# Halving six expert answers on VectorE ahead of the transposes, and normalizing layer 0's output on ScalarE

## The chip, the cores and the metric

The kernel runs on one core of a Trainium2 chip. The time is device microseconds from start to end of one execution, as a median of several runs. The engines of the core work in parallel, each through its own list of instructions in order: TensorE (PE) for matrix products and transposes, VectorE (DVE), ScalarE (ACT), GpSimd (POOL) and SyncE (SP), which here only issues transfers.

## What is computed

The reference has two layers on 8192 tokens (128 graphs of 64 nodes) with 256 values each. Each layer is a graph convolution and then a mixture of experts. Only the seam between the layers matters here: what layer 0 does with its six expert answers per token, and all of layer 1's convolution.

```
# layer 0, experts: six of 64 are chosen for a token, scores are their softmax
lattice_out = einsum('bske,bsk->bse', xW, scores)      # six answers, weighted and summed
proj = einsum('bsd,ed->bse', lattice_out, out_w) + out_b
h = x + proj                                           # x: the layer-normed input
ffn = (h - mu) * rsqrt(var + 1e-5) * ln_g + ln_b
x = x_residual + ffn
# layer 1, convolution, on layernorm(x)
h = layer_norm(xn, ln_gamma, ln_beta)
agg = einsum('bij,bjh->bih', adj, h)
x = x + (xn + relu(agg @ W_rel + b_rel + h @ W_root))
# layer 1, experts: two of eight are chosen, then each token's two answers are added
```

## The kernel before

The program has four stages, one after the other:

1. **layer 0's convolution and routing**: each token is written six times into a table in memory, sorted by expert;
2. **layer 0's experts**: pages of 128 rows go through their expert's matrix, are scaled with their score and scattered to `r0.answer`, six rows of 256 values to a token;
3. **the fused pass**: it reads the six answers of each token, adds them up, finishes layer 0, does layer 1's convolution and routes the tokens to layer 1's experts;
4. **layer 1's experts**.

The change is in stage 3 alone. It works in 32 blocks of 256 tokens (two tiles `t` of 128 tokens; a tile's tokens lie on the 128 partitions). The function `staggered` writes the program out as a software pipeline: in step s it calls each function of the list, in the list's order, for block s minus its lag. So step s has `mixture` and `out_proj` of block s+1, `layer_out_h`, `_a`, `_b`, `_c` of block s, `flip_h`, `neighbours`, `convolve_a`, `convolve_b` of block s-1, `residual1_a`, `residual1_b`, `flip3`, `gate1` of block s-2, and `choose1`, `count1`, `place1` of block s-3. Steps 3 to 30 have all of them; those before and after have a part.

For PE, VectorE and ScalarE the order of the program is the order of execution (`manual_schedule`). The issues on SP and POOL are ordered by a scheduler, and each queue works in its order.

What one block goes through, with the lines of the profile:

- `load3` (L801): SP loads the six answers `y` (L804, 1536 KB, two buffers), the normed input `xn1` (L806), the residual `x1` (L808), three buffers each, and two blocks of the adjacency (L492).
- `mixture` (L811): 24 transposes on PE (L818), six to each of the four 128x128 squares of the PSUM tile, the six adding up there, so that sum and transpose are one. ScalarE copies the result to `accT` (L821).
- `out_proj` (L823): one bias product (L826) and the product with `out_w` on PE (L829) into the one buffer `po`.
- `layer_out_h` (L835): VectorE adds `xn1` and gives `h`. `layer_out_a`: VectorE takes mean and variance of `h` (L45, L46, two tiles), ScalarE the root of the variance (L36), and VectorE adds `ln_b` to `x1` (L841).
- `layer_out_b`: on VectorE the reciprocal of the root (L847) and then for each tile two operations on 128x256 elements: L850 takes off the mean and multiplies by `ln_g`, L852 multiplies by the reciprocal and adds `x1`, which gives `x2`. Statistics of `x2` follow (L45, L46) and two roots on ScalarE (L36).
- `layer_out_c`: scale and shift on VectorE (L67, L68, twice, and L866), four operations on ScalarE (`hn` L869, `s` L873).
- `flip_h` (L76, `hT` L882), `neighbours` (L890, `z` L893), `convolve_a` (L898, L901 into the one buffer `pc`) and `convolve_b` (L907): PE, with ScalarE emptying PSUM.
- `residual1_a`: L913 on VectorE gives `x3`, SP writes it out (L914), statistics, root. `residual1_b`: scale and shift on VectorE (L67, L68), then ScalarE writes `xs` (L923, two operations of 512 elements to a partition).
- `flip3` (L76, `xn3T` L930), `gate1` (L936, into the one buffer `pg`), `choose1` (L942, L178 to L183, L251), `count1` (L191), `place1` (L267 to L281), and four scattering transfers from POOL (L287).

The order on VectorE within a step is so: `choose1` (L942 first), `residual1_a`, `layer_out_a`, `residual1_b`, `layer_out_b`, `place1`, `layer_out_c`, and then `layer_out_h` of the next step's block, which its list has first.

`scale_shift` (L62 to L69), which the change calls once more, is the pair of small VectorE operations L67 and L68: the reciprocal of the root, and minus the mean times it.

Of the kernel before, what the change touches and what calls it, by code (L numbers as in the profile page):

```python
# [9 lines left out]
F32 = mybir.dt.float32  # L10
# [5 lines left out]
AF = mybir.ActivationFunctionType  # L16
ALU = mybir.AluOpType
AX = mybir.AxisListType
PSUM = bass.MemoryType.PSUM
P = 128  # L20
# [382 lines left out]
def staggered(n, stages, first=0):  # L403

    for s in range(first + min(lag for lag, _ in stages), n + max(lag for lag, _ in stages)):
        for lag, f in stages:
            if first <= s - lag < n:
                f(s - lag)
# [3 lines left out]
def two_layer_gnn_moe_kernel(ctx: ExitStack, tc: tile.TileContext, a: dict, out: bass.AP):  # L412
    nc = tc.nc
    x_in, adjT = a["x"], a["adjT"]
    N, D = x_in.shape
# [4 lines left out]
    T = 2  # L420
    C = T * P
# [4 lines left out]
    K0 = 6  # L426
# [15 lines left out]
    ops = Ops(nc, small, ident, eps)  # L442

    def load_rows(pool, name):
        t = pool.tile([P, a[name].shape[0]], F32, name="r_" + name)
        nc.scalar.dma_start(out=t, in_=rows_of(a[name]))
        return t
# [31 lines left out]
    def by_tile(ap):  # L479
        return ap.rearrange("(t p) d -> p t d", p=P)  # L480
# [8 lines left out]
    def load_adjacency(b):  # L489
        at = adjacency[b % 4]  # L490
        for g in range(2):
            nc.sync.dma_start(out=at[g * G:(g + 1) * G, :, g * G:(g + 1) * G],  # L492
                              in_=adjT[2 * b * T + g:2 * (b + 1) * T:2].rearrange("t m n -> m t n"))
        return at
# [3 lines left out]
    r0 = Router(tc, const, small, dram, N, D, E0, K0, T, P, 14 * P, 4, "r0")  # L498
# [22 lines left out]
    with tc.tile_pool(name="c0", bufs=1) as c0, \  # L521
# [9 lines left out]
        blocks = [dict() for _ in range(NB)]  # L531
# [247 lines left out]
    with tc.tile_pool(name="c3", bufs=1) as c3, \  # L779
# [5 lines left out]
        ln_g = load_rows(c3, "L0_ffn_ln_g")  # L785
# [11 lines left out]
        blocks = [dict() for _ in range(NB)]  # L797
        pg = pmix.tile([P, T, E1], F32, name="pg")
        r1.begin(counts, work, pmix.tile([P, 2, T, E1], F32, name="pos"))

        def load3(b):  # L801
            B = blocks[b]
            B["y"] = y = work.tile([P, T, K0, D], F32, name="y")
            nc.sync.dma_start(out=y, in_=r0.answer[ts(b, C * K0), :].rearrange("(t p k) d -> p t k d", p=P, k=K0))  # L804
            B["xn1"] = xn1 = work.tile([P, T, D], F32, name="xn1", bufs=3)
            nc.sync.dma_start(out=xn1, in_=by_tile(xn1_dram[b]))  # L806
            B["x1"] = x1 = work.tile([P, T, D], F32, name="x1", bufs=3)
            nc.sync.dma_start(out=x1, in_=by_tile(x1_dram[b]))  # L808
            B["at"] = load_adjacency(b)

        def mixture(b):  # L811

            B = blocks[b]
            pt = psum.tile([P, KD, C], F32, name="ps")
            for k in range(KD):
                for t in range(T):
                    for i in range(K0):
                        nc.tensor.matmul(pt[:, k, ts(t, P)], lhsT=B["y"][:, t, i, ts(k, P)], rhs=ident,  # L818
                                         start=(i == 0), stop=(i == K0 - 1), is_transpose=True)
            B["accT"] = accT = work.tile([P, KD, C], F32, name="accT", bufs=1)  # L820
            nc.scalar.copy(accT, pt)  # L821

# [14 lines left out]
        def layer_out_a(b):  # L837
# [2 lines left out]
            B["rsh"] = ops.spread(B["mvh"])  # L840
            nc.vector.tensor_add(B["x1"], B["x1"], ln_b.unsqueeze(1).to_broadcast([P, T, D]))  # L841

        def layer_out_b(b):
            B = blocks[b]
            h = B["h"]
            mv, rs = B["mvh"], B["rsh"]
            nc.vector.reciprocal(rs, rs)  # L847
            B["x2"] = x2 = work.tile([P, T, D], F32, name="x2")
            for t in range(T):
                nc.vector.scalar_tensor_tensor(h[:, t, :], h[:, t, :], mv[:, t, 0:1], ln_g,  # L850
                                               op0=ALU.subtract, op1=ALU.mult)
                nc.vector.scalar_tensor_tensor(x2[:, t, :], h[:, t, :], rs[:, t:t + 1], B["x1"][:, t, :],  # L852
                                               op0=ALU.mult, op1=ALU.add)
            B["mv2"] = mv = ops.stats(x2)
            B["std2"] = ops.spread(mv)


            B["rs2"] = rs2 = small.tile([P, T], F32, name="rs2")
            ops.std(rs2, mv[:, :, 1], 1e-10, 1.0 + 1e-5)
# [93 lines left out]
        def place1(b):  # L953
            B = blocks[b]
            r1.send(r1.places(b, B["hot"]), B["xs"])

        staggered(NB, (
            (-2, load3),
            (0, layer_out_h),
            (3, choose1),  # L960
            (-1, mixture),
            (1, flip_h),
            (3, count1),
            (2, residual1_a),
            (0, layer_out_a),
            (-1, out_proj),
            (2, residual1_b),
            (1, neighbours),
            (0, layer_out_b),
            (1, convolve_a),  # L970
            (2, flip3),
# [106 lines left out]
```

## Time and profile before

| | us |
|---|---|
| median of 3 runs (2194.39 to 2196.17) | 2195.01 |
| the profiled execution | 2200.25 |
| its span, on which all views below count | 2198.1 |
| stage 1, up to about | 630 |
| stage 2, up to about | 1264 |
| fused pass: first steps, up to L942 of step 3 | 1313.32 |
| fused pass: steps 3 to 30, up to L942 of step 31 | 1629.51 |
| fused pass: last steps, up to stage 4's first transpose | 1672.9 |
| stage 4, up to the end | 2198.1 |

Between the stretch of steps 3 to 30 and the sum over the whole span, the engines were busy so (us):

| | PE | VectorE | ScalarE | POOL |
|---|---|---|---|---|
| whole span | 1945.1 | 1186.6 | 1015.9 | 1182.8 |
| steps 3 to 30 (316.19 us) | 316.19 | 277.15 | 199.75 | 117.41 |

A busy time is the time in which at least one instruction of the engine was under way. An instruction that needs nothing of the one ahead of it may begin before that one has ended, so that a row's mean duration is longer than what the instruction adds to a row of them. The distance between two starts is told in the text as such. The granted clock ("PEclk") is the share of its full speed that PE was given in a stretch.

### The profile page before, as it was taken

What the parts mean: (1) busy time and instruction counts of PE and PEld (TensorE: products, weight loads), DVE (VectorE), ACT (ScalarE), POOL (GpSimd) and SP (SyncE); (2) the same over time, 40 slices, a digit from 0 to 9 for tenths busy, and PEclk for the clock granted to TensorE, in tenths of its full rate; (3) what the DMA queues carried; (4) which work ended last, traced back from release to release, by engine and by line L of the source; (5) the groups of instructions that cost most, each with busy time, mean ns of one, the idle gap of its engine ahead of it and who ended that gap; (6) DMA issues with size and microseconds to landing.
All of it is one profiled execution on the core that took longest, in us unless ns stands there. A gap on an engine that the chain in (4) does not pass through costs nothing. (4 is left out here: it accounts for less than half of the span.)

```text
span 2198.1 us, 37431 instructions
## 1 busy us (share of the span) xinstructions
PE 1945.1 (88%) x10563; PEld 1684.8 (77%) x10564; DVE 1186.6 (54%) x3904; ACT 1015.9 (46%) x2037; POOL 1182.8 (54%) x1178
## 2 busy tenths in 40 slices
PE   3999999999961988998898479999996999999997
PEld 2888888888851877887777368888875888888886
DVE  4688888888873333333333248888882222222221
ACT  2887887777750222222222036666662333333332
POOL 1166676666655777777777703333343444434444
PEclk9999999999985999999999789999997999999999
DMA  8143334443364988767675379888835776666665
GB/s 247 56 133 123 129 131 134 133 133 134 127 214 136 282 254 256 210 202 206 206 206 170 92 277 316 265 265 267 262 124 142 179 170 158 162 157 161 162 160 117
DMA packets 283580, 398.93 MB, mean 181 GB/s; under 512 B 56024, under 2 KB 237416, under 8 KB 283376
## 3 DMA queue, kind: packets, MB, share of 16 engines
q1 hardware_dynamic: 200736, 246.15, 38.3%
q0 software_dynamic: 64800, 136.14, 20.8%
q10 hardware_dynamic: 17840, 14.21, 2.0%
q8 instruction: 93, 1.52, 0.3%
q14 instruction: 111, 0.91, 0.2%
HBM read 223.89 MB, written 177.69 MB: 183 GB/s over the span
## 5 line engine op out<-in xcount | busy, mean ns | idle before, releaser
L287 POOL DMA_INDIRECT r0x<-xs,r0row x384 | 397.7, 1036 | 222.2 <-DVE lat L613 100.7
L294 POOL DMA_INDIRECT r0y<-py_s,px x424 | 417.6, 985 | 143.7 <-DMA r0y<-py_s,px 58.2
L758 PE MATMUL py<-lat,pxT 128*128 x1696 | 411.0, 385 | 40.0 <-DVE py_s L763 22.5
L763 DVE TENSOR_SCALAR py_s<-py,px 128x256 f32<-128x256 f32 x424 | 185.6, 479 | 377.4 <-DMA r0y<-py_s,px 158.5
L302 POOL DMA_INDIRECT out_x<-py_s,px x138 | 214.4, 1554 | 312.1 <-DMA out_x<-py_s,px 184.2
L758 PEld LDWEIGHTS py<-lat,pxT 128*128 128x128 f32 x1696 | 307.2, 191 | 91.0 <-issue 31.2
L745 ACT COPY pxT<-pt 128x512 f32<-128x512 f32 x212 | 124.0, 586 | 440.8 <-PE pt L743 309.5
L1017 ACT ACTIVATE phid<-ph,pw 128x256 f32<-128x256 f32 x276 | 131.0, 475 | 325.3 <-issue 178.4
L1015 PE MATMUL ph<-pxT,pw 128*128 128x256 f32 x1104 | 251.4, 381 | 2.1 <-DMA pw<-in_L_ffn_W1b 2.1
L1034 PE MATMUL py<-fw,phid 128*128 x1104 | 249.9, 379 | 0.6 <-ACT phid L1017 0.6
L591 PE MATMUL ph<-lat 128*128 128x256 f32 x1024 | 233.2, 387 | 17.8 <-DVE lat L613 17.1
L624 PE MATMUL ps<-lat 128*128 128x256 f32 x1024 | 237.1, 380 | 0.0
L1015 PEld LDWEIGHTS ph<-pxT,pw 128*128 128x128 f32 x1104 | 211.0, 191 | 31.4 <-issue 2.5
L591 PEld LDWEIGHTS ph<-lat 128*128 128x128 f32 x1024 | 195.2, 193 | 46.9 <-DVE lat L613 17.4
L1034 PEld LDWEIGHTS py<-fw,phid 128*128 128x128 f32 x1104 | 204.4, 190 | 26.0 <-ACT phid L1017 1.0
L624 PEld LDWEIGHTS ps<-lat 128*128 128x128 f32 x1024 | 192.8, 191 | 24.5
L287 POOL DMA_INDIRECT r1x<-xs,r1row x128 | 129.8, 1014 | 115.7 <-ACT xn3T L930 61.9
L743 PE MATMUL pt<-ident,px 128*128 128x128 f32 x848 | 131.8, 277 | 45.0 <-DMA px<-r0x 44.7
L743 PEld LDWEIGHTS pt<-ident,px 128*128 128x128 f32 x848 | 106.8, 143 | 70.9 <-issue 42.9
L1028 DVE TENSOR_SCALAR p<-p 128x2 f32<-128x2 f32 x69 | 12.0, 174 | 240.1 <-ACT p L1027 240.1
L1037 DVE TENSOR_TENSOR py_s<-py,pb 128x512 f32<-128x512 f32 x69 | 47.7, 692 | 157.0 <-PE py L1034 152.0
L615 ACT ACTIVATE lat<-lat,c_L_gnn_rms_weight 128x256 f32<-128x256 f32 x256 | 105.6, 495 | 47.8 <-DVE lat L613 47.7
(264 smaller groups left out, 2866.7 us busy)
## 6 DMA issues: line engine op xcount, KB each, us to landing
px<-r0x SPq DMA_DIRECT2D x424, 129.0 KB
y<-r0y SPq DMA_DIRECT2D x32, 1536.0 KB
pw<-in_L_ffn_W1b SPq DMA_DIRECT2D x69, 514.0 KB
px<-r1x SPq DMA_DIRECT2D x69, 258.0 KB
x<-x SPq DMA_DIRECT2D x64, 256.0 KB
pb<-in_L_ffn_b SPq DMA_DIRECT2D x69, 128.0 KB
r0x<-r0filler ACTq DMA_DIRECT2D x64, 129.0 KB
lat<-in_x SPq DMA_DIRECT2D x32, 256.0 KB
```

The lines of the kernel that those rows point to most:

```text
L287: i = self.nc.gpsimd.indirect_dma_start(out=self.table[:, :], out_offset=bass.IndirectOffsetOnAxis(ap=row[:, t, k:k + 1], axis=0), in_=xs[ ...
L294: i = self.nc.gpsimd.indirect_dma_start(out=self.answer[:, :], out_offset=bass.IndirectOffsetOnAxis(ap=x[:, self.D:self.D + 1].bitcast(I32 ...
L302: i, d = f"{self.name}add{i}", self.nc.gpsimd.indirect_dma_start(out=self.total[:, :], out_offset=bass.IndirectOffsetOnAxis(ap=x[:, self.D ...
L591: nc.tensor.matmul(ph[:, c, :], lhsT=w1[:, k, ts(2 * j + c, P)], rhs=B["aggT"][:, k, :], start=(k == 0), stop=(k == KD - 1))
L624: nc.tensor.matmul(B["po"][:, t, :], lhsT=B["hT"][:, c, ts(t, P)], rhs=w2[:, c, :], start=False, stop=(t == T - 1 and c == KH - 1))
L743: nc.tensor.transpose(pt[:, k, ts(q, P)], Q["px", q][:, 0, ts(k, P)], ident)
L745: nc.scalar.copy(xT[:, :, :n * P], pt[:, :, :n * P])
L758: nc.tensor.matmul(py[:, q, :], lhsT=Q["xT"][:, k, ts(q, P)], rhs=lat[:, ds(regs["e"][(2 * j + q) % 4], 1), k, :].rearrange("p o d -> p (o ...
L763: nc.vector.tensor_scalar(y[:, q, :], py[:, q, :], px[:, 0, D + 1:D + 2], None, op0=ALU.mult)
L1015: nc.tensor.matmul(ph, lhsT=w[:, k * F1 + c * P:k * F1 + (c + 1) * P], rhs=Q["xT"][:, k, :], start=(k == 0), stop=(k == KD - 1))
L1017: nc.scalar.activation(hid[:, c, :], ph, AF.Relu, bias=w[:, KD * F1 + c:KD * F1 + c + 1], scale=1.0)
L1034: nc.tensor.matmul(py[:, t, :], lhsT=Q["hid"][:, c, ts(t, P)], rhs=fw2[:, ds(regs["e"][i % 4], 1), c, :].rearrange("p o d -> p (o d)"), st ...
```

## The change

`load_y` takes the load of `y` out of `load3` and issues it one step earlier, with three buffers in place of two. `halve`, a new VectorE operation in each step, adds answers 3 to 5 of a block to its answers 0 to 2, in place: 2 x 768 elements on each partition in one instruction. `mixture` then transposes and sums three answers in place of six. `layer_out_n`, also new, forms scale and shift of `h` on VectorE (`scale_shift`) and lets ScalarE normalize `h` in place, a tile at a time. `layer_out_b` has one multiplication by `ln_g` and one addition of `x1`, each over both tiles (128x512), where it had a reciprocal and four operations on 128x256. In the list `layer_out_n` stands behind `residual1_b`, and `halve`, for block s+2, stands behind `neighbours` and right ahead of `layer_out_b`.

```
--- before.py
+++ after.py
@@ -798,10 +798,16 @@
         pg = pmix.tile([P, T, E1], F32, name="pg")
         r1.begin(counts, work, pmix.tile([P, 2, T, E1], F32, name="pos"))
 
+        def load_y(b):
+            blocks[b]["y"] = y = work.tile([P, T, K0, D], F32, name="y", bufs=3)
+            nc.sync.dma_start(out=y, in_=r0.answer[ts(b, C * K0), :].rearrange("(t p k) d -> p t k d", p=P, k=K0))
+
+        def halve(b):
+            y = blocks[b]["y"]
+            nc.vector.tensor_add(y[:, :, :K0 // 2, :], y[:, :, :K0 // 2, :], y[:, :, K0 // 2:, :])
+
         def load3(b):
             B = blocks[b]
-            B["y"] = y = work.tile([P, T, K0, D], F32, name="y")
-            nc.sync.dma_start(out=y, in_=r0.answer[ts(b, C * K0), :].rearrange("(t p k) d -> p t k d", p=P, k=K0))
             B["xn1"] = xn1 = work.tile([P, T, D], F32, name="xn1", bufs=3)
             nc.sync.dma_start(out=xn1, in_=by_tile(xn1_dram[b]))
             B["x1"] = x1 = work.tile([P, T, D], F32, name="x1", bufs=3)
@@ -814,9 +820,9 @@
             pt = psum.tile([P, KD, C], F32, name="ps")
             for k in range(KD):
                 for t in range(T):
-                    for i in range(K0):
+                    for i in range(K0 // 2):
                         nc.tensor.matmul(pt[:, k, ts(t, P)], lhsT=B["y"][:, t, i, ts(k, P)], rhs=ident,
-                                         start=(i == 0), stop=(i == K0 - 1), is_transpose=True)
+                                         start=(i == 0), stop=(i == K0 // 2 - 1), is_transpose=True)
             B["accT"] = accT = work.tile([P, KD, C], F32, name="accT", bufs=1)
             nc.scalar.copy(accT, pt)
 
@@ -840,17 +846,19 @@
             B["rsh"] = ops.spread(B["mvh"])
             nc.vector.tensor_add(B["x1"], B["x1"], ln_b.unsqueeze(1).to_broadcast([P, T, D]))
 
+        def layer_out_n(b):
+            B = blocks[b]
+            h = B["h"]
+            rs, nm = ops.scale_shift(B["mvh"], B["rsh"])
+            for t in range(T):
+                nc.scalar.activation(h[:, t, :], h[:, t, :], AF.Identity, bias=nm[:, t:t + 1], scale=rs[:, t:t + 1])
+
         def layer_out_b(b):
             B = blocks[b]
             h = B["h"]
-            mv, rs = B["mvh"], B["rsh"]
-            nc.vector.reciprocal(rs, rs)
             B["x2"] = x2 = work.tile([P, T, D], F32, name="x2")
-            for t in range(T):
-                nc.vector.scalar_tensor_tensor(h[:, t, :], h[:, t, :], mv[:, t, 0:1], ln_g,
-                                               op0=ALU.subtract, op1=ALU.mult)
-                nc.vector.scalar_tensor_tensor(x2[:, t, :], h[:, t, :], rs[:, t:t + 1], B["x1"][:, t, :],
-                                               op0=ALU.mult, op1=ALU.add)
+            nc.vector.tensor_mul(h, h, ln_g.unsqueeze(1).to_broadcast([P, T, D]))
+            nc.vector.tensor_add(x2, h, B["x1"])
             B["mv2"] = mv = ops.stats(x2)
             B["std2"] = ops.spread(mv)
 
@@ -955,6 +963,7 @@
             r1.send(r1.places(b, B["hot"]), B["xs"])
 
         staggered(NB, (
+            (-3, load_y),
             (-2, load3),
             (0, layer_out_h),
             (3, choose1),
@@ -965,7 +974,9 @@
             (0, layer_out_a),
             (-1, out_proj),
             (2, residual1_b),
+            (0, layer_out_n),
             (1, neighbours),
+            (-2, halve),
             (0, layer_out_b),
             (1, convolve_a),
             (2, flip3),
```

In the changed kernel's lists of instructions each step of PE has 12 transposes fewer. VectorE's order within a full step is: `choose1`, `residual1_a`, `layer_out_a`, the pair L67, L68 of `residual1_b`, the same pair of `layer_out_n`, the halving, the multiplication, the addition, the statistics of `x2`, `place1`, `layer_out_c`, `layer_out_h`. ScalarE's is: `accT`, `hT` twice, two roots, `xs` twice, the two normalizations of `h`, `z`, two roots, `xn3T`, `hn` twice, `s` twice.

More of the change, by code (lines that the diff above doesn't have):

```diff
@@ L799, in two_layer_gnn_moe_kernel, with load_y, halve @@
         r1.begin(counts, work, pmix.tile([P, 2, T, E1], F32, name="pos"))
+        def load_y(b):
+            blocks[b]["y"] = y = work.tile([P, T, K0, D], F32, name="y", bufs=3)
+            nc.sync.dma_start(out=y, in_=r0.answer[ts(b, C * K0), :].rearrange("(t p k) d -> p t k d", p=P, k=K0))
+        def halve(b):
+            y = blocks[b]["y"]
+            nc.vector.tensor_add(y[:, :, :K0 // 2, :], y[:, :, :K0 // 2, :], y[:, :, K0 // 2:, :])
         def load3(b):
             B = blocks[b]
-            B["y"] = y = work.tile([P, T, K0, D], F32, name="y")
-            nc.sync.dma_start(out=y, in_=r0.answer[ts(b, C * K0), :].rearrange("(t p k) d -> p t k d", p=P, k=K0))
             B["xn1"] = xn1 = work.tile([P, T, D], F32, name="xn1", bufs=3)
@@ L816, in mixture @@
                 for t in range(T):
-                    for i in range(K0):
+                    for i in range(K0 // 2):
                         nc.tensor.matmul(pt[:, k, ts(t, P)], lhsT=B["y"][:, t, i, ts(k, P)], rhs=ident,
-                                         start=(i == 0), stop=(i == K0 - 1), is_transpose=True)
+                                         start=(i == 0), stop=(i == K0 // 2 - 1), is_transpose=True)
             B["accT"] = accT = work.tile([P, KD, C], F32, name="accT", bufs=1)
@@ L841, in layer_out_a, with layer_out_n @@
             nc.vector.tensor_add(B["x1"], B["x1"], ln_b.unsqueeze(1).to_broadcast([P, T, D]))
+        def layer_out_n(b):
+            B = blocks[b]
+            h = B["h"]
+            rs, nm = ops.scale_shift(B["mvh"], B["rsh"])
+            for t in range(T):
+                nc.scalar.activation(h[:, t, :], h[:, t, :], AF.Identity, bias=nm[:, t:t + 1], scale=rs[:, t:t + 1])
         def layer_out_b(b):
@@ L845, in layer_out_b @@
             h = B["h"]
-            mv, rs = B["mvh"], B["rsh"]
-            nc.vector.reciprocal(rs, rs)
             B["x2"] = x2 = work.tile([P, T, D], F32, name="x2")
[L849 to L853, printed above, removed]
+            nc.vector.tensor_mul(h, h, ln_g.unsqueeze(1).to_broadcast([P, T, D]))
+            nc.vector.tensor_add(x2, h, B["x1"])
             B["mv2"] = mv = ops.stats(x2)
@@ L957, in two_layer_gnn_moe_kernel @@
         staggered(NB, (
+            (-3, load_y),
             (-2, load3),
@@ L967, in two_layer_gnn_moe_kernel @@
             (2, residual1_b),
+            (0, layer_out_n),
             (1, neighbours),
+            (-2, halve),
             (0, layer_out_b),
```

## The prediction

> **What bounds the kernel now.** First the 40 slices, to see where the fused pass lies and how full each engine is there.
>
> ```profile
> PE   3999999999961988998898479999996999999997
> DVE  4688888888873333333333248888882222222221
> ```
>
> A slice is 54.95 us, so slices 24 to 29 are the pass: PE is full, and VectorE at 8 tenths is not far behind. Second, the steady part alone, from L942 of step 3 to L942 of step 31 (columns: us, then busy us and instructions of PE, PE's weight loads, VectorE, ScalarE, POOL; granted clock, DMA share, GB/s).
>
> ```profile
> 1313.32:1629.51 316.19, 316.19 (x2074) 277.13 (x2073) 277.15 (x1232) 199.75 (x421) 117.41 (x136) 1.00 0.79 260
> ```
>
> 28 steps, 316.19 / 28 = 11.29 us each, with PE busy for all of it. VectorE is busy for 9.90 us of a step. Whether the other 1.39 us are free is what decides this case, so third VectorE's groups in twenty of these steps (busy us, mean ns; then idle time ahead of them and its cause), with one group from stage 1.
>
> ```profile
> L852 DVE SCALAR_TENSOR_TENSOR x<-h,bn_sd,x 128x256 f32<-128x256 f32 x40 | 19.4, 485 | 1.4
> L850 DVE SCALAR_TENSOR_TENSOR h<-h,bn_mv,r_L_ffn_ln_g 128x256 f32<-128x256 f32 x40 | 18.9, 472 | 0.0
> L841 DVE TENSOR_TENSOR x<-x,r_L_ffn_ln_b 128x512 f32<-128x512 f32 x20 | 13.2, 658 | 0.0
> L942 DVE TENSOR_TENSOR logits<-pg,r_L_ffn_bg 128x16 f32<-128x16 f32 x20 | 3.5, 175 | 12.5 <-PE pg L936 12.5
> ...
> L601 DVE TENSOR_TENSOR lat<-lat 128x1024 f32<-128x1024 f32 x27 | 33.7, 1249 | 22.9 <-ACT lat L594 22.9
> ```
>
> Only L942 waits for another engine: 12.5 / 20 = 0.63 us in a step, for `gate1`. The rest of the 1.39 us are seams between small dependent operations that come again in any order. VectorE's list is therefore 11.29 - 0.63 = 10.67 us long, against PE's 11.29: it is the next bound, and 0.63 us is all it can take.
>
> Fourth, one step in order of time (start, us). I count from L942 at 1437.53 as zero.
>
> ```profile
> 1442.75 0.16 DVE L68 SCALAR_TENSOR_TENSOR bn_nm<-bn_mv,bn_rs 128x2 f32<-128x2 f32 x1
> 1442.83 0.16 DVE L847 RECIPROCAL bn_sd<-bn_sd 128x2 f32<-128x2 f32 x1
> 1442.90 0.46 DVE L850 SCALAR_TENSOR_TENSOR h<-h,bn_mv,r_L_ffn_ln_g 128x256 f32<-128x256 f32 x1
> ...
> 1444.72 0.42 DVE L45 BATCH_NORM_STATS2 bn_st<-x 128x6 f32<-128x256 f32 x1
> ...
> 1447.51 0.69 DVE L835 TENSOR_TENSOR h<-po,xn 128x512 f32<-128x512 f32 x1
> ```
>
> ```profile
> 1443.00 1.52 ACT L923 ACTIVATE xs<-x,bn_nm,bn_rs 128x512 f32<-128x512 f32 x2 [0.60 <-DVE bn_nm L68]
> 1444.71 0.59 ACT L893 COPY z<-pz 128x512 f32<-128x512 f32 x1 [0.20 <-PE pz L890]
> ...
> 1447.09 0.59 ACT L930 COPY xn3T<-ps 128x512 f32<-128x512 f32 x1 [0.63 <-PE ps L76]
> 1447.58 1.09 ACT L869 ACTIVATE hn<-x,bn_nm,bn_rs 128x256 f32<-128x256 f32 x2
> ```
>
> L68 of `residual1_b` ends at 5.38, the statistics of `x2` (L45) begin at 7.19, L835 ends at 10.67. ScalarE starts `xs` as soon as L68 is done and is busy with it until 6.99.
>
> **The change part by part.** *PE*: 24 transposes take 2.67 us (chain view, L818), so 12 give back 1.33: PE's step becomes 9.96 us. Since VectorE can only give 0.63 of that back before it binds, the other 0.70 are worth nothing as they stand.
>
> *VectorE, the four operations*: from L850's start to L45's is 1.82 us. In their place stand a multiplication and an addition on 128x512, each dependent on the one before; L841 has that form at 0.66, and a dependent follower starts 0.04 after the end (L850 to L852: 0.50 for 0.46). 2 x 0.70 = 1.40, a gain of 0.42. *Scale and shift of h*: the pair L67, L68 takes 0.27 from start to start here, in place of one reciprocal at 0.07: a loss of 0.20.
>
> *The halving*: 1536 elements to a partition, an operation that the trace does not have. From below: L841's 658 ns for 512 and 393 ns for the 256 of L563 give 265 per 256, so 1.72 us. From above: L601's 1249 for 1024 and 699 for 512 give 550 per 512, so 1.80. It is L601's kind of addition, but without that one's chain; I take 1.75. Its successor can start 0.08 before its end, as L67 does behind L841.
>
> *The new wait*: the multiplication needs `h` from ScalarE, and in ScalarE's list the two normalizations come behind both `xs`. `xs` still starts at 5.47 and blocks until about 6.95; two operations of the form of L869 take 1.09; `h` is there at 8.05. On VectorE the pair of `layer_out_n` ends its issue at 5.57 and the halving lasts to 7.32, so VectorE stands for 0.73 us. The halving is thus wholly hidden under ScalarE's 5.47 to 8.05, and would be up to 2.48 us; without that cover it costs 1.67. Behind the waiting multiplication are queued the statistics of `x2`, `place1` (POOL's sends wait for it, but POOL is busy for 117.41 / 28 = 4.2 us of a step), `layer_out_c` (`hn`, next step's `flip_h`), `layer_out_h` and the next L942.
>
> So: multiplication at 8.05, addition 8.75, statistics 9.45 in place of 7.19, that is 2.26 later, and VectorE's list ends at 10.67 + 2.26 = 12.93. That is the new step, if nothing else ends later. The other candidate is the way to L942 by PE: last statistics done at 10.61, both roots on ScalarE, which stand ahead of `xn3T` in its list, `xn3T` 11.10 to 11.69, `gate1` 1.06, L942 at 12.84. The two are level, VectorE ahead by 0.1. ScalarE's step grows by 1.09 to 8.2 us and does not bind.
>
> *PE's clock*: PE now has about 3 us of gaps in a step, the largest, some 2.2 us, ahead of `gate1`. What gaps do shows at the end of the pass (same columns as above):
>
> ```profile
> 1630.00:1631.00 1.00, 0.00 (x0) 0.00 (x0) 0.88 (x8) 1.00 (x3) 0.76 (x1) 1.00 0.38 128
> ...
> 1632.00:1633.00 1.00, 1.00 (x4) 0.79 (x3) 0.93 (x5) 0.00 (x0) 0.70 (x2) 0.50 0.39 139
> ```
>
> After 1.05 us without work the granted clock went to 0.50 for some 3.3 us; after 0.82 and 0.71 us again. A `gate1` at half clock (1657.17) took 1.88 in place of 1.06, and by the way over PE a step would then be 13.66, 0.73 more. Bounds: nothing (clock stays, or drops after `gate1`) to 0.73 in every step. A gap of 2.2 us must pull the clock down in most steps, but a slow PE also closes its own gap in the next step; I take 0.3. The Trainium skill, "TensorE: Matmul & The Clock Gate", section "Why this matters for your kernels", advises against PE-idle gaps above about 3 us between bursts, since a whole idle window throttles. By that rule the 2.2 us would cost nothing and the sum would be 8 us lower; the rows above, where 1.05 us sufficed, speak against it.
>
> *Loads*: SP issues as many transfers as before, `y` a step earlier. With three buffers one is free when `mixture` of three blocks before is done, and the halving needs it two steps and 4 us later, some 30 us; the slowest `y` in the chain view landed in 7.84 us. The DMA share of 0.79 falls with a longer step. Nothing, where it was covered before too. In the first steps `y` binds; the halving there delays (1.75), fewer transposes and an earlier `y` of block 2 advance: zero, by -2 to +2.
>
> **Sum.** Steps 3 to 30: 28 x (12.93 - 11.29) = 45.9. Clock: 28 x 0.3 = 8.4. Step 31 (10.63 us now, no halving, but the same wait): 12.84 - 10.63 = 2.2. Together 56.5 us, a span of 2198.1 + 56.5 = 2254.6. The profiled execution's span is 3.1 above the median of the runs, so the median is 2195.0 + 56.5 = 2251.5; I say 2251.
>
> **Rivals.** *A, ScalarE's part hides*: the normalizations are ready when the halving ends. The multiplication then starts at 7.24, statistics at 8.64, and the step is 12.12: 28 x 0.83 + 1.4 = 25, so 2220. For it: ScalarE stands idle for 0.60 us ahead of `xs`, so its list is not full there. Against it: that idle time ends with the very L68 that `xs` needs, and `xs`, 1.5 us long, is ahead of the normalizations in a list that is kept in order. *B, faster*: VectorE's additions, halving included, fit into the 0.63 us that L942 waits, and PE's relief shows: at most 28 x 0.63 = 17.6 less, 2177. It needs less than 0.63 more on VectorE's list and my rows give 2.26; L841 would have to be off threefold. *C, the clock dominates*: every `gate1` at half clock, and the slow stretch (half of 3.3 us lost) at worst not covered: 0.73 to 1.6 in a step, 2263 to 2288. For it: `gate1` directly follows the gap. Against it: PE has 3 us of slack for all but `gate1`. *D, the edit has no effect on time*, since what PE gains VectorE loses: it would need 0.63 sharp.
>
> **Numbers.** Forecast 0.72, A 0.12, C 0.11, B 0.04, D 0.01. A measurement of this kernel tells about 0.2% from no change. The bounds of the unknown clock alone span 2243 to 2264; half of A's and C's cases added, 2222 to 2270. Slower 0.94, faster 0.04, same 0.02.
>
> **What would show it.** In the changed profile's steady steps: a distance of 12.9 to 13.4 us between L950s (the old L942); PE busy about 10 us of it; the multiplication L860 waiting some 0.7 us for ScalarE's `h`, and the halving at 1.7 to 1.8. A step near 12.1 with L860 not waiting is A; stretches of granted clock 0.5 in each step with L950 waiting for `gate1` are C; L950 still waiting for a PE that is busy throughout is B. I am wrong if VectorE's list can be packed closer than its start-to-start distances before.

## The result, and the profile after

| | before | after |
|---|---|---|
| median, us (range, runs) | 2195.59 (2194.39 to 2197.61, 4) | 2250.22 (2247.74 to 2258.79, 4) |
| ratio of after to before, 95% interval | | 1.0255 [1.0225, 1.0285] |
| profiled execution / its span | 2200.25 / 2198.1 | 2258.79 / 2257.0 |
| L942 (after: L950) of step 3 | 1313.32 | 1311.92 |
| the same of step 31 | 1629.51 | 1676.18 |
| steps 3 to 30 / mean step | 316.19 / 11.29 | 364.26 / 13.01 |
| step 31 | 10.63 | 12.80 |

The kernel is 2.55% slower. The forecast was 2251. First the 40 slices of the page; the third row is the clock granted to PE.

```profile
PE   3999999999934989998997388888886999999997
DVE  4688888888872333333333388888882222222221
PEclk9999999999966999999999698989887999999999
```

The fused pass is now about slices 23 to 30, of 56.4 us each. PE has gone from full to 8 tenths, and its clock has dents; VectorE has not become fuller in exchange: it stood at 8 tenths before and stands there now. Neither engine is full, so the pass is held by waits between engines. The steady part alone, from L950 of step 3 to L950 of step 31 (us, then busy us and instructions of PE, PE's weight loads, VectorE, ScalarE and POOL; granted clock, DMA share, GB/s):

```profile
1311.92:1676.18 364.26, 318.50 (x1737) 272.83 (x1735) 317.87 (x1232) 226.94 (x476) 113.74 (x136) 0.90 0.71 222
```

Here are 48.07 us more than before in 28 steps. VectorE is busy 317.87 / 28 = 11.35 us of a mean step of 13.01, and PE 11.37: fewer instructions of PE (1737 in place of 2074) take as long as before, at a mean clock of 0.90 in place of 1.00. VectorE's groups in 19 of these steps (busy us, mean ns; then idle time ahead of them and its cause):

```profile
L807 DVE TENSOR_TENSOR y<-y 128x1536 f32<-128x1536 f32 x19 | 33.3, 1751 | 0.0
L860 DVE TENSOR_TENSOR h<-h,r_L_ffn_ln_g 128x512 f32<-128x512 f32 x19 | 13.1, 692 | 13.0 <-ACT h L854 13.0
L861 DVE TENSOR_TENSOR x<-h,x 128x512 f32<-128x512 f32 x19 | 13.1, 692 | 0.6
```

Of the three wide operations only the multiplication L860 waits, 13.0 / 19 = 0.68 us in a step, and it waits for ScalarE. The order of time of one step shows why; first VectorE, then ScalarE in the same step (start, duration, then the idle time ahead).

```profile
1447.26 0.16 DVE L68 SCALAR_TENSOR_TENSOR bn_nm<-bn_mv,bn_rs 128x2 f32<-128x2 f32 x1
1447.34 1.75 DVE L807 TENSOR_TENSOR y<-y 128x1536 f32<-128x1536 f32 x1
1449.78 0.69 DVE L860 TENSOR_TENSOR h<-h,r_L_ffn_ln_g 128x512 f32<-128x512 f32 x1 [0.69 <-ACT h L854]
1450.51 0.69 DVE L861 TENSOR_TENSOR x<-h,x 128x512 f32<-128x512 f32 x1
1451.23 0.43 DVE L45 BATCH_NORM_STATS2 bn_st<-x 128x6 f32<-128x256 f32 x1
...
1454.03 0.69 DVE L841 TENSOR_TENSOR h<-po,xn 128x512 f32<-128x512 f32 x1
1454.63 0.17 DVE L950 TENSOR_TENSOR logits<-pg,r_L_ffn_bg 128x16 f32<-128x16 f32 x1
```

```profile
1447.24 1.53 ACT L931 ACTIVATE xs<-x,bn_nm,bn_rs 128x512 f32<-128x512 f32 x2 [0.54 <-DVE bn_rs L67]
1448.67 1.08 ACT L854 ACTIVATE h<-h,bn_nm,bn_rs 128x256 f32<-128x256 f32 x2
```

ScalarE does both `xs` (L931, until 1448.8) and then both tiles of `h` (L854, until 1449.75). VectorE has the halving in the meantime and then stands; L860 starts as soon as `h` is there. This step began with L950 at 1441.79 and the next L950 starts at 1454.63: 12.84 us.

### The profile page after: what moved, and what is told of

It reads as the page before. It is cut to its first block, busy times and chain, and to the rows that moved or that the text cites. A ratio compares the mean times of both kernels' runs of the same rounds, so it can differ in the third digit from the quotient of the medians.

```text
span 2257.0 us, 36820 instructions
## 1 busy us (share of the span) xinstructions
PE 1945.7 (86%) x10178; PEld 1674.7 (74%) x10180; DVE 1233.1 (55%) x3904; ACT 1046.7 (46%) x2101; POOL 1177.3 (52%) x1178
## 4 chain that ended last, share of the span: by engine, by line
DMA 29%; PE 20%; DVE 9%; issue 5%; POOL 4%; ACT 3%; SPq 0%; POOLq 0%; DVEq 0%; ACTq 0%
DMA r0y<-py_s,px 19%; DMA out_x<-py_s,px 7%; PE py L1045 6%; PE ph L1026 6%; DVE bn_st L45 2%; POOL out_x L302 2%; PE py L758 2%; POOL r0x L287 1%; ACT xs L931 1%; ACT h L854 1%; PE pg L944 1%; PE pz L898 1%; DVE bn_mv L46 1%; PE po L835 1%; DVE x L861 1%
## 5 line engine op out<-in xcount | busy, mean ns | idle before, releaser
L1048 DVE TENSOR_TENSOR py_s<-py,pb 128x512 f32<-128x512 f32 x69 | 47.7, 691 | 169.2 <-PE py L1045 120.3
```

## The experiments

The theory: a step is VectorE's list in its order (taken as 10.67 us before), lengthened by the halving, and beyond that by the wait for a `h` that ScalarE makes only behind `xs`. Each figure below is for the stretch from L950 of step 3 to that of step 31 (or the line that L950 is in that kernel), and every ratio is against the kernel before on the same chip.

| kernel | median, us | ratio | typical (median) / mean step |
|---|---|---|---|
| the change | 2250.22 | 1.0255 [1.0225, 1.0285] | 12.85 / 13.01 |
| 1 halving alone | 2233.52 | 1.0162 [1.0145, 1.0179] | 12.30 / 12.35 |
| 2 norm on ScalarE alone | 2255.06 | 1.0256 [1.0239, 1.0273] | 12.85 or 13.9 / 13.26 |
| 3 norm ahead of `xs` | 2226.40 | 1.0125 [1.0108, 1.0143] | 12.11 / 12.26 |
| 4 one more addition | 2253.92 | 1.0261 [1.0242, 1.0280] | 12.86 / 13.04 |
| 5 halving on GpSimd | 2253.78 | 1.0252 [1.0232, 1.0272] | mean 13.22 |
| 6 halving on GpSimd, norm on ScalarE | 2302.32 | 1.0475 [1.0457, 1.0492] | mean 14.55 |
| 7 norm reordered, no halving | 2206.04 | 1.0035 [1.0022, 1.0047] | 11.53 / 11.52 |
| 8 halving in the transfer | 2245.67 | 1.0218 [1.0197, 1.0239] | mean 12.49 |
| 9 the same, more `xs` buffers | 2188.34 | 0.9964 [0.9951, 0.9978] | 10.49 / 10.55 |

**1. The halving alone.** The norm goes back to VectorE; `halve` and its 12 transposes stay.

```
-        def layer_out_n(b): ...
-            nc.vector.tensor_mul(h, h, ln_g.unsqueeze(1).to_broadcast([P, T, D]))
-            nc.vector.tensor_add(x2, h, B["x1"])
+            nc.vector.reciprocal(rs, rs)
+            ... (for each tile, the two scalar_tensor_tensor of before)
-            (0, layer_out_n),
```

> The halving and the 12 transposes stay; the normalization of h goes back to VectorE as in the kernel before (one reciprocal, four operations on 128x256), so VectorE waits for nobody. Theory (VectorE's list in order, its waits included, is the step): 10.67 + 1.67 for the halving = 12.34 us between two of the logits additions, no wait ahead of them but for some late gate products; the median about 2195 + 28 x 1.05 + some 5 for PE's clock = 2229. Rival 1 (the sum of VectorE's work decides, its wait for h costs nothing since other work would fill it): about as slow as the changed kernel or slower, 2250, since four narrow operations are 0.2 us dearer than what replaces them. Rival 2 (PE's clock is the cost): half clock in each step as in the changed kernel and 2245 to 2250.

Measured 2233.52. Ten of the 28 steps lie at 12.24 to 12.27 us, which is 10.59 + 1.67: step 30, the one that has no halving because there is no block 32, is 10.59 us long, and in it VectorE waits for nobody. Its two ends:

```profile
1647.68 0.16 DVE L948 TENSOR_TENSOR logits<-pg,r_L_ffn_bg 128x16 f32<-128x16 f32 x1
...
1658.27 0.17 DVE L948 TENSOR_TENSOR logits<-pg,r_L_ffn_bg 128x16 f32<-128x16 f32 x1
```

VectorE's list is thus 10.59 long, 0.08 shorter than taken. Three more steps are a little shorter, the rest longer by late gates (in 8 steps VectorE waits for one, 2.80 us in sum), and it is by them that the mean, 12.35, comes to the 12.34 of the forecast. The halving is paid in full by VectorE; of its 1.67 us the 0.63 that VectorE used to wait for `gate1` are gained back, and PE's saving is worth no more than that.

**2. The norm on ScalarE alone.** No halving, six answers transposed again.

```
-                    for i in range(K0 // 2):
+                    for i in range(K0):
...
-            (-2, halve),
```

> No halving, 24 transposes as in the kernel before; ScalarE normalizes h and VectorE has the two wide operations, as in the changed kernel. VectorE has 0.22 us less to do than in the kernel before, PE the same. Theory: the multiplication still waits for ScalarE until 8.05 us into the step, now with some 2.35 us of waiting where the halving was, so the step is 12.84 us as in the changed kernel, with the clock of PE full; median 2195 + 28 x 1.55 + 2 = 2240. Rival 1 (VectorE's work decides): step 11.29, 2195 or a little less. Rival 2 (PE's clock): 2195 as well, since PE has no gaps.

Measured 2255.06, level with the whole change (1.0256 against 1.0255), although VectorE has the largest addition less: over the 28 steps it is busy for 272.27 us, less than before (277.15). So the time is in the wait and not in the work of VectorE. The wait is larger by what the halving had covered, here in VectorE's waits over these steps (us in sum, times, longest):

```profile
DVE h L860 <- ACT h L854: 65.7, 28, 2.4
DVE bn_rs L67 <- ACT bn_sd L36: 10.5, 11, 1.2
```

65.7 / 28 = 2.35 us in every step. The forecast of this run, 2240, was still 15 too low. By 4.5 of them the kernel before was slower on this chip too; the rest is the second row, a wait that 11 steps had and that was not foreseen. One of these steps in order of time, first PE, then ScalarE:

```profile
1377.75 1.06 PE L944 MATMUL pg<-m_L_ffn_Wg,xn3T 128*128 128x8 f32 x8 [1.41 <-ACT xn3T L938]
1378.67 4.48 PE L824 MATMUL ps<-ident,y 128*128 128x128 f32 x24
```

```profile
1383.24 0.58 ACT L827 COPY accT<-ps 128x512 f32<-128x512 f32 x1 [3.23 <-PE ps L824]
1384.63 0.48 ACT L36 ACTIVATE bn_sd<-bn_mv,eps 128x2 f32<-128x2 f32 x2
```

After an idle time of 1.41 us the 24 transposes take 4.48 us (in the step ahead of it 2.82). `accT` comes that much later, and in ScalarE's list it stands ahead of the roots (L36) that VectorE's L67 needs, so a slow PE stops VectorE. Of the 28 steps 17 take about 12.85 us, the other 11 about 13.9. The granted clock (third value from the end) over the transposes of the step ahead, over this gate and over these transposes:

```profile
1365.83:1368.48 2.65, 2.65 (x26) 2.65 (x26) 2.43 (x14) 1.34 (x3) 2.04 (x3) 1.00 0.66 181
...
1377.75:1378.60 0.85, 0.85 (x8) 0.85 (x9) 0.78 (x5) 0.67 (x2) 0.15 (x1) 1.00 0.30 68
```

```profile
1378.67:1383.10 4.43, 4.43 (x28) 4.43 (x28) 4.10 (x20) 1.34 (x3) 3.52 (x4) 0.61 0.47 150
```

1.00, 1.00 and 0.61: the clock fell behind the gate. That the gap ahead of it is the cause is inferred from the order of time.

**3. The norm ahead of `xs`.** One line of the list moves, nothing else.

```
-            (2, residual1_b),
             (0, layer_out_n),
+            (2, residual1_b),
```

> The changed kernel with one line of the stage list moved: scale, shift and normalization of h go ahead of those of x3, so that ScalarE writes h before xs. Work is the same on every engine. Theory: h is there before the halving ends, the multiplication does not wait, and the step is 12.84 - 0.68 = 12.16 us; median about 2250 - 28 x 0.68 = 2231, or some us lower with fewer late gate products. Rival 1 (VectorE's work decides, the wait would be made up for elsewhere): no change, 2250. Rival 2 (xs is needed on the way to the gate, and a later xs makes it late): 2250 to 2260, with the wait moved to the logits addition.

Measured 2226.40, a typical step 12.11 (forecast 12.16). On VectorE the halving and the multiplication now touch:

```profile
1440.96 1.75 DVE L807 TENSOR_TENSOR y<-y 128x1536 f32<-128x1536 f32 x1
1442.62 0.69 DVE L860 TENSOR_TENSOR h<-h,r_L_ffn_ln_g 128x512 f32<-128x512 f32 x1
```

L860 follows 1.66 us after the halving's start with no wait in brackets. The steps without a late gate take 12.09, and 12.84 - 12.09 = 0.75: the wait of 0.68 is worth its full length, and the multiplication now also starts 0.08 ahead of the halving's end. This is also the prediction's rival A put on the chip, with its step of 12.12. The mean step is 12.26, because in 8 steps the gate is late (3.64 us in sum).

**4. One more wide addition.** Behind each halving a dead addition of 512 elements to a partition, whose result nobody reads.

```
+        spare = c3.tile([P, T, D], F32, name="spare")
...
+            nc.vector.tensor_add(spare, spare, ln_b.unsqueeze(1).to_broadcast([P, T, D]))
```

> The changed kernel with one more addition of 128x512 behind each halving, into a tile that nothing reads (0.58 to 0.66 us of VectorE in each step). Theory: it falls into VectorE's wait of 0.68 us for h, the step stays at 12.84 us and L860's wait shrinks to about 0.1 us; median as the changed kernel's, 2250. Rival 1 (VectorE's work decides): 28 x 0.6 = 17 us more, 2267.

Measured 2253.92, a mean step of 13.04 against the change's 13.01. VectorE:

```profile
1449.60 1.75 DVE L809 TENSOR_TENSOR y<-y 128x1536 f32<-128x1536 f32 x1
1451.26 0.69 DVE L810 TENSOR_TENSOR spare<-spare,r_L_ffn_ln_b 128x512 f32<-128x512 f32 x1
1452.03 0.69 DVE L863 TENSOR_TENSOR h<-h,r_L_ffn_ln_g 128x512 f32<-128x512 f32 x1
```

The addition fills the time in which VectorE stood, and costs next to nothing: the 28 steps take 365.07 us in place of 364.26. The rival, by which each operation on VectorE is paid (17 us more), is out.

**5. The halving on GpSimd.** Experiment 1's kernel, with one word changed.

```
-            nc.vector.tensor_add(y[:, :, :K0 // 2, :], ...
+            nc.gpsimd.tensor_add(y[:, :, :K0 // 2, :], ...
```

> The run with the halving alone, but the halving is on GpSimd in place of VectorE; 12 transposes, normalization on VectorE as in the kernel before. Theory: VectorE's list is the 10.67 us of the kernel before, PE's 9.96, so VectorE is the bound with 10.7 to 10.9 us in a step (late gate products included), 11 to 17 us less than before in steps 3 to 30, if one GpSimd addition of 1536 elements takes less than the 5 us that GpSimd has left in a step; the first steps may give 3 us back. Rival 1: GpSimd's addition takes longer than it has time for and becomes the bound, step above 11.29. Rival 2: VectorE's own operations get slower while GpSimd adds, so that its list is longer than 10.67 with the same operations; their mean durations then show it.

Measured 2253.78: worse than with VectorE's own addition (2233.52). The second rival held. VectorE's addition of `ln_b` is 658 ns long in the kernel before (group L841 there). Here it is the group below, in 16 steps, and one of its cases is shown beside GpSimd's addition (POOL, then VectorE):

```profile
L847 DVE TENSOR_TENSOR x<-x,r_L_ffn_ln_b 128x512 f32<-128x512 f32 x16 | 37.9, 2370 | 0.0
```

```profile
1401.09 3.43 POOL L807 TENSOR_TENSOR y<-y 128x1536 f32<-128x1536 f32 x1
```

```profile
1400.99 0.18 DVE L46 BATCH_NORM_AGGREGATE bn_mv<-bn_st 128x2 f32<-128x6 f32 x1
1401.09 3.98 DVE L847 TENSOR_TENSOR x<-x,r_L_ffn_ln_b 128x512 f32<-128x512 f32 x1
1405.00 0.15 DVE L67 RECIPROCAL bn_rs<-bn_sd 128x2 f32<-128x2 f32 x1
```

Both begin at 1401.09. GpSimd's ends at 1404.52, VectorE's at 1405.07, 0.55 later: it has stood still for nearly all of it. The steps are uneven, from 10.57 to 16.5 us.

**6. Both: GpSimd's halving and the norm on ScalarE**, with `layer_out_n` ahead of `residual1_b` and `place1` ahead of `layer_out_b`, so that VectorE has work while ScalarE normalizes.

```
-            nc.vector.tensor_add(y[:, :, :K0 // 2, :], ...
+            nc.gpsimd.tensor_add(y[:, :, :K0 // 2, :], ...
...
+            (0, layer_out_n),
             (2, residual1_b),
-            (0, layer_out_n),
             (1, neighbours),
             (-2, halve),
+            (3, place1),
             (0, layer_out_b),
...
-            (3, place1),
```

> Halving on GpSimd; ScalarE normalizes h ahead of xs, and place1 stands ahead of layer_out_b, so that VectorE has 0.97 us of other work while ScalarE normalizes. Theory: VectorE's list is 10.67 - 0.42 + 0.20 = 10.45 us without a wait, PE's 9.96: step 10.45 to 10.7, 3 to 6 us below the run with the halving on GpSimd alone. Rivals as there.

Measured 2302.32, the slowest of all, and the expectation is missed as in run 5. L860 waits no more in the steady steps, yet most of them are 15.03 us long. VectorE and POOL show the cause, here in six steps and in one of them:

```profile
L181 DVE CAST r1which<-r1idx 128x4 f32<-128x4 uint32 x6 | 22.8, 3797 | 0.2
```

```profile
1510.85 3.79 DVE L181 CAST r1which<-r1idx 128x4 f32<-128x4 uint32 x1
```

```profile
1511.18 3.42 POOL L807 TENSOR_TENSOR y<-y 128x1536 f32<-128x1536 f32 x1
```

A conversion of four numbers to a partition, 174 ns long in the kernel before, lasts until GpSimd's addition ends. 15.03 less the 11.53 of the next run, which has the same order, no addition and all 24 transposes, is 3.50: GpSimd's whole addition, 3.42 us long, stands in VectorE's list.

**7. The norm reordered, without the halving.** The order of run 6, 24 transposes, no `halve`.

> No halving, 24 transposes; ScalarE normalizes h ahead of xs, place1 ahead of layer_out_b. VectorE's list 10.45 us, no wait for h. Theory: PE is the bound again with 11.29 us, the granted clock full, and the time is that of the kernel before within 0.3%: moving the normalization costs nothing once VectorE has other work in its place, and what VectorE saves is worth nothing under a PE bound. Rival (the wide forms or ScalarE's operations cost something by themselves): step above 11.29.

Measured 1.0035 [1.0022, 1.0047], just outside what was expected. Moving the norm to ScalarE costs almost nothing when VectorE has other work meanwhile: in the steady steps L860 waits no more. But the work taken as cover had been cover elsewhere, as VectorE's waits show:

```profile
DVE bn_rs L67 <- ACT rs L36: 17.1, 28, 0.6
```

`place1` used to stand between the roots of `x2` and the L67 that needs them; without it L67 waits 17.1 / 28 = 0.61 us in each step. ScalarE's round trip was shifted and in part covered, not removed. The step of 11.53 in place of 11.29 is set on another way, which the same shift lengthens. Here is ScalarE in a step that starts at 1450.03, and below it `xn3T` in a step of the kernel before that starts at 1448.83:

```profile
1459.66 0.28 ACT L36 ACTIVATE rs<-bn_mv,eps 128x2 f32<-128x2 f32 x1
1459.85 0.56 ACT L938 COPY xn3T<-ps 128x512 f32<-128x512 f32 x1
```

```profile
1458.39 0.59 ACT L930 COPY xn3T<-ps 128x512 f32<-128x512 f32 x1 [0.62 <-PE ps L76]
```

With `place1` ahead of it the statistics of `x2` end later, and so do the roots, which stand ahead of `xn3T` in ScalarE's list. `xn3T` starts 9.82 us into the step in place of 9.56, and the gate comes 0.24 later by it. VectorE's own list, wait included, would have let L950 start at about 11.35 (0.61 behind L841, which starts at 10.74).

**8. The halving in the transfer.** Experiment 1's kernel, in which SP loads three answers and a second transfer, issued by POOL, adds the other three to them as it lands. VectorE's list is thus that of the kernel before, and PE has 12 transposes fewer.

```
+            nc.sync.dma_start(out=y, in_=rows[:, :, :K0 // 2, :])
...
-            nc.vector.tensor_add(y[:, :, :K0 // 2, :], ...
+            nc.gpsimd.dma_start(out=y, in_=rows[:, :, K0 // 2:, :], accum_op=ALU.add)
```

> Nobody's engine halves: SP loads the first three answers of each token, and a GpSimd transfer adds the last three onto them while it writes (768 KB each); 12 transposes, normalization on VectorE as in the kernel before. Theory: VectorE's list is the 10.67 us of the kernel before and PE's 9.96, so VectorE is the bound with 10.7 to 10.9 us in a step, late gate products included; 28 x 0.4 to 0.6 = 11 to 17 us below the kernel before, less some us in the first steps, where a block now needs two transfers one after the other. Rival 1: the adding transfer is slow or its issue holds GpSimd up, so that the transposes wait for y: step above 11.29. Rival 2: writing its descriptors stretches VectorE's operations as the addition on GpSimd did: L847 well above 0.66 us.

This run fell on another chip, on which the kernel before takes 2477.96; the ratio there is 1.0026 [1.0007, 1.0045], where 11 to 17 us less were expected. So the same kernel was run once more on a chip like the others':

> The kernel with the halving in the transfer once more, because the chip of its first run was 13% slower for the kernel before as well (2478 us), in the stages with scattered transfers above all. There its steps lay between 10.5 us, as forecast, and 14.5 us, with GpSimd waiting for the landing of earlier sends (L249 for the scatter of L287). On a chip on which the kernel before takes 2195 to 2200 us, theory: the transfers are faster, most steps 10.6 to 10.9 us and 5 to 15 us less than the kernel before. Rival: the adding transfers share GpSimd's queue with the sends, and the waits of some steps make it no faster than the kernel before.

Measured 2245.67, and the rival held: steps between 10.5 and 16.2 us. The long ones wait for the sends, here POOL's and ScalarE's waits in the window 1320 to 1600 (us in sum, times, longest):

```profile
POOL xs L249 <- DMA r1x<-xs,r1row: 98.3, 18, 6.5
ACT xs L931 <- DMA r1x<-xs,r1row: 30.9, 12, 5.7
```

POOL and ScalarE want to write the next `xs` while all its buffers still wait for their sends to land; behind `xs` waits `xn3T`, and with it the gate. That the adding transfers are what delays the sends is inferred: POOL's queue took 47.7% of the transfer engines' time in this window, and 12.2% in the kernel before.

**9. The same with five `xs` buffers.**

```
-            B["xs"] = xs = work.tile([P, T, 2, W], F32, name="xs", bufs=3)
+            B["xs"] = xs = work.tile([P, T, 2, W], F32, name="xs", bufs=5)
```

> As the kernel with the halving in the transfer, with five buffers of xs in place of three, so that ScalarE, VectorE and GpSimd write xs without waiting for the landing of the sends of three blocks before. Theory: if that wait makes the long steps, they come down to 10.6 to 10.9 us and the time lies 3 to 10 us below the kernel with three buffers. Rival: the DMA engines themselves are full, the steps stay long and the waits move to y.

Measured 2188.34, 0.9964 [0.9951, 0.9978]: the only one of these kernels that beats the kernel before, by 0.4%. It is 57 us faster than run 8, where 3 to 10 were expected: that the buffers were what the long steps waited for was right, what the waits cost was far underestimated. The steady part, with the columns of the first such row:

```profile
1316.55:1612.03 295.48, 283.19 (x1737) 240.31 (x1735) 273.79 (x1233) 198.88 (x420) 153.22 (x163) 1.00 1.00 275
```

295.48 against 316.19 us: 20.7 saved, most steps 10.47 to 10.63 us, with no wait at the gate, so VectorE's list alone. PE is busy for 96% of it and keeps its clock. 3.2 us are given back ahead of it, where `y` binds and now takes two transfers (step 3 begins at 1316.55 in place of 1313.32), and 4.8 in stage 4, whose code is the same (526.8 us in place of 522.0); the spans differ by 13.3 us and the medians by 8.9. The DMA share is 1.00: by this measure the transfers have no room left. Five buffers in the kernel before were not run; PE, which was busy there for all of the 316.19 us, would still have bound it.

## Why the prediction was right, point by point

**What bounds it.** Right. VectorE's list was the next bound and had 0.63 to take before the change: in run 1 the halving's 1.67 is paid on top of the list. The list itself was taken 0.08 too long, 10.67 in place of 10.59.

**The halving.** 1.75 us, as taken; its successor starts 1.66 later, as taken from the seams of the rows before.

**The four operations.** 0.69 each in place of 0.66, 0.72 from start to start where 0.70 was taken. With that, and with the pair L67, L68, the norm on ScalarE should shorten VectorE's list by 0.42 - 0.04 - 0.20 = 0.18; the steps without a late gate in runs 1 and 3 give 12.26 - 12.09 = 0.17.

**The new wait.** Right in place, cause and size: 0.73 forecast, 0.68 in the rows, 0.75 by the steps of run 3. Without the halving as cover 2.35, where the bound was 2.48.

**The step.** 12.84 typical against 12.93. Up to the statistics of `x2` the sum holds: they begin 9.44 us into the step, 2.25 later than before, where 2.26 was taken. The rest is the end of the list: the sum counted L841 (L835 before) to its end, but the next L950 starts 0.60 behind L841's start, while L841 (0.69 long) is still under way. In the kernel before, L942 waited for the gate, and this seam could not be seen. 28 x (12.84 - 11.29) = 43.4 us, forecast 45.9.

**PE's clock.** This term was mis-sized: 8.4 us taken, 0.3 in a step; all that the 28 steps have above 12.84 is 364.26 - 359.5 = 4.7, or 0.17 in a step. 2.9 of them are waits for the gate. Its mechanism is as told, but rarer: the prediction let the gap pull the clock down in most steps, and 21 of the 28 gates took their 1.06 us, the other 7 from 1.15 to 1.88. In most steps the gate comes in time, and in 6 VectorE waits for it:

```profile
DVE logits L950 <- PE pg L944: 2.9, 6, 0.7
```

Two gates ran at half clock throughout. Here is one of them; the gate and the transposes of the step ahead of it stand first for comparison:

```profile
1544.23 1.06 PE L944 MATMUL pg<-m_L_ffn_Wg,xn3T 128*128 128x8 f32 x8 [1.33 <-ACT xn3T L938]
1545.14 1.51 PE L824 MATMUL ps<-ident,y 128*128 128x128 f32 x12
...
1557.08 1.88 PE L944 MATMUL pg<-m_L_ffn_Wg,xn3T 128*128 128x8 f32 x8 [2.11 <-ACT xn3T L938]
```

1.88 in place of 1.06, the price that the row of before had given, at a granted clock of 0.50:

```profile
1557.08:1558.80 1.72, 1.72 (x8) 1.72 (x9) 1.14 (x5) 1.55 (x4) 0.98 (x2) 0.50 0.33 95
```

The bound of 0.73 in every step was not reached, because in 22 of 28 steps VectorE does not wait for the gate at all. The clock is low in PE's other work too (0.90 in the mean), and that has slack. One of the signs named was wrong by it: PE was to be busy for about 10 us of a step and is for 11.37. PE's saving itself was right, 2.82 - 1.51 = 1.31 us by the transposes' rows at full clock (24 of them in run 2, 12 here) where 1.33 was taken; but a mean clock of 0.90 takes 0.10 x 13.01 = 1.3 us of a step.

**The other terms.** First steps -1.4 (forecast 0, by -2 to 2). Step 31 +2.17 (2.2); L860 waits 2.35 there, since no halving covers it. The remaining last steps give 1.1 more, which was not in the sum. With the 48.07 of the steady steps this makes 50.0 us up to the first product of stage 4, where 56.5 were forecast. The medians differ by 54.6. The rest lies within stage 4, whose code is unchanged, and which took 531.0 us in this profiled execution and 522.0 in that of before; in the profiles of the experiments it took 519.9 to 529.9 (531.2 on the slower chip of run 8). So part of the total's closeness is luck: 6.5 us too much in the pass, met by a difference of about that size in a stage that was left alone. Whether the change adds anything to stage 4 stays open.

**The rivals.** A (12.12) needed the other order, run 3. B fell: PE's relief was worth 0.63 a step and the halving cost 1.67. C asked for every gate at half clock: two were, and in 6 steps of 28 VectorE waited for a gate. D is out, by 2.55%.

**The rule on gaps.** The Trainium skill, "TensorE: Matmul & The Clock Gate", section "Why this matters for your kernels", advises against PE-idle gaps of more than about 3 us between bursts, since a whole idle window throttles. In these rows shorter gaps were followed by a lower clock: behind a gap of 2.11 us the gate ran at a clock of 0.50 here, and some 0.9 us behind one of 1.41 us in run 2 the transposes did so at 0.61.

## What to carry to other kernels

An engine that runs its list in order pays for every operation moved away from it with a round trip: before moving work, count where the other engine's list stands at that moment, and what fills the time until the answer is there. Work removed from the engine that binds is worth no more than the distance to the next one (here 0.63 us), and work added to an engine that stands is free up to the length of its wait (run 4). If the next bound is an engine, look for a third place for the work, and then for what that place's queue holds up: here the transfers could add, once `xs` had buffers enough.

## What the runs showed of the hardware

**GpSimd stops VectorE's operations with two operands in SBUF.** L847, both of whose operands lie there, went from 658 to 2370 ns in the mean, and the case shown lasts until 0.55 us after GpSimd's addition has ended (run 5). In the 10 of the 28 steps in which the two meet it took 2.88 to 4.14 us, in the others 0.66. Another case of run 5, GpSimd first and then VectorE, shows an operation that is not stopped beside one that is:

```profile
1462.69 3.46 POOL L807 TENSOR_TENSOR y<-y 128x1536 f32<-128x1536 f32 x1
```

```profile
1464.10 0.17 DVE L270 TENSOR_TENSOR r1place<-pos,r1run 128x16 f32<-128x16 f32 x1
1464.30 1.90 DVE L277 TENSOR_TENSOR r1prod<-r1hot,r1place 128x32 f32<-128x32 bf16 x1
```

L270 reads `pos` from PSUM and takes its usual 0.17 us; L277 has both operands in SBUF and ends 0.05 us behind GpSimd's addition, after 1.90 us in place of 0.19. The statistics with their one operand are not stopped either (0.39 to 0.42 us in the cases that fall into an addition). The conversion L181, with its single small operand, is (174 ns before, 3797 in run 6). The Trainium skill, "SBUF — State Buffer", section "SBUF: two separate sides", describes an exclusive lock between GpSimd and VectorE that is held for a whole instruction; of VectorE's operations it meets those with two SBUF inputs, if GpSimd's operation reads SBUF, and those in a two-port mode. The rows of L847, L270 and L277 agree; that L181 runs in such a mode no row shows. GpSimd needed 3.43 us for what VectorE does in 1.75.

**Transfers that add do not stop VectorE.** In run 9 the same addition of `ln_b` took 659 ns. What stood beside them were other transfers: POOL waited for the sends of `xs` for up to 6.5 us (run 8).

**PE's clock fell where each step left PE idle for more than a microsecond.** Ahead of the gate PE stood for up to 2.1 us in the changed kernel (41.7 us in the 28 steps) and for up to 1.4 in run 2 (33.7 us); the mean clock was 0.90 and 0.95, and in run 2 eleven steps of 28 took a microsecond more. In run 9, with at most 0.7 us there (12.2 us), and in the kernel before, where PE did not stand at all, it stayed at 1.00. Within the changed kernel the clock was either 1.00 or 0.50, and each slow stretch was 3.4 or 6.8 us long, as from 1556.9 to 1563.7; so not every gap has a slow gate behind it. That the gaps are the cause is inferred from these pairs.

**A chip can be slower in a part of the program.** The kernel before took 2477.96 us on one chip and about 2197 on the others. The kernel of run 8, profiled on both kinds, reached step 3 at 1569.37 us there and at 1317.71 here, so that the whole difference of some 250 us lies ahead of it, while its steps 3 to 30 took 336.71 us there and 349.58 here. For that reason every ratio above is taken on one chip.
